# Layer 2's attention in an eight-block transformer kernel: the sums of weights taken one row a head, inverted there and spread by a product

## The chip, the core and the metric

The kernel runs on one core of a Trainium2 chip. The time is the device time of one execution, in microseconds (us); the lower the better. A core has a matmul engine (TensorE, PE in the profile, with its weight loads as PEld), a vector engine (VectorE, DVE), a scalar engine (ScalarE, ACT), a general engine (GpSimd, POOL) and an engine that issues transfers (SyncE, SP). Each takes its instructions from a list of its own, in order; they wait for each other by semaphores. SBUF is the memory on the chip, PSUM the small memory that TensorE writes to, in eight banks of 128 x 512 float32.

## The reference

All of it is float32. The input `x` has 128 sequences of 64 tokens of 128 numbers (8192 tokens), with a context of the same 128 x 64 tokens of 96 numbers. Eight blocks follow each other (four attentions, four feed-forward layers), each added to `x` through a gate. The change touches one, layer 2's attention with 16 heads of 8 numbers, which sees a normalised `x` as `query` and the context as `key_value`:

```python
q = (query @ Wq + bq).reshape(B, Nq, H, D).transpose(0, 2, 1, 3)
k = (key_value @ Wk + bk).reshape(B, Nkv, H, D).transpose(0, 2, 1, 3)
v = (key_value @ Wv + bv).reshape(B, Nkv, H, D).transpose(0, 2, 1, 3)
attn = jnp.einsum('bhqd,bhkd->bhqk', q, k) * scale
attn = jnp.clip(attn, -CLAMP, CLAMP)
attn = jax.nn.softmax(attn, axis=-1)
attn = jnp.where(jnp.any(jnp.isnan(attn)), jnp.asarray(1.0 / Nkv, attn.dtype), attn)
x = jnp.einsum('bhqk,bhkd->bqhd', attn, v).reshape(B, Nq, Cq)
return x @ Wo + bo
```

Each sequence attends to its own 64 context tokens. The softmax's division is done late in the kernel: the weights are exponentials, the products with `v` are taken of these, and what comes out is divided by the sum of the weights of its head and query.

## The kernel before, in words

`l2_cross` (from line 788) is a software pipeline written out by hand. A unit `u` is four sequences, 256 tokens ("a pair" of token tiles; 32 of them, `NP`); a group `g` is two units (16, `NG`). `PLAN` (line 967) is the order of work in one period; `period(i)` goes through it and calls each step for unit `i + lag`, the steps of kind "g" only where that number is even, for group (i + lag) / 2. All engines' instructions are recorded through `InOrder` (line 158), which ties each to the one before it on its engine, so `PLAN` is the order on every engine. Line 166 issues them all, so the profile names that line for every instruction, and one goes by the names of the tiles.

The steps of one period `i`, with what each puts on which engine:

- `count` and `clamp` (unit i): ACT takes a sum of exponentials of the raw scores `sc`, to see later whether any is not a number; DVE clamps the scores from PSUM into `s`, in two halves.
- `norm` (unit i+4): ACT normalises two tiles into `xn`; for odd units POOL then adds the gated bias to `x`.
- `heads` (unit i-3): TensorE multiplies the turned weights `aT` with `vz`, which holds the values of each head in otherwise empty columns, into the left half (256 columns) of a bank `pso`: row 8h+d is head h, number d, and the columns are the 256 tokens. Then it multiplies `aT` with `hot_v`, ones at the places of a head, into the right half: there all eight rows of a head get the same sum.
- `qk` (group of even i): projections `psq`, `psk`, copied by ACT to `qT`, `kT`.
- `power` (unit i-1): ACT's exponential of `s`, in two halves.
- `values` (unit i-2): projection `psv`. `turn` (unit i-2), halves 0 and 1: TensorE transposes the weights, two banks `psa` a half; ACT copies each to `aT`. Between the halves `scores` (unit i+1) on TensorE, from `qT` and `kb`.
- `transposes` (odd i): `psx`, copied by ACT to `xT`.
- `largest` (unit i): DVE's maximum `m` of each row of `s`; `less` (unit i): POOL subtracts it, in two halves.
- `place` (unit i-2): DVE copies `psv` into `vz` (two copies).
- `spread` (unit i+2): POOL makes `kb`, each key repeated by head under a mask, in two halves.
- `divide` (unit i-3): DVE inverts the right half of `pso` (128 x 256) to `rec` and multiplies the left half with it into `oT_all`.
- `statistics` (even i): DVE's mean and variance of four tiles, then four small steps on POOL (`rs`, `rr`, `nb` twice).

So even periods have `qk` and `statistics`, odd ones `transposes` and the bias. The `pso`, `psq`, `psk`, `psv`, `psa` and `psx` tiles share four banks of PSUM (`bank`, line 63), each taken by the next tile when its last user is done; the scores have the other four.

After the last scores three more periods empty the pipeline; between them `groups` puts the output projection `psf` and its addition to `x`, and `ahead` runs the first steps of the next layer. `l2_ffn` (line 1037) follows: 32 experts with top-8 routing, whose router's small tiles `m8`, `gt`, `eq` have two buffers each.

```python
        PLAN = [
            ("u", 0, count, 0), ("u", 0, clamp, 1), ("u", 4, norm), ("u", 0, clamp, 0), ("u", 0, count, 1),
            ("u", -3, heads), ("g", 2, qk), ("u", -1, power, 0), ("u", -1, power, 1),
            ("u", -2, values), ("u", -2, turn, 0), ("u", 1, scores), ("u", -2, turn, 1), ("g", 3, transposes),
            ("u", 0, largest), ("u", 0, less, 0), ("u", 0, less, 1), ("u", -2, place), ("u", 2, spread),
            ("u", -3, divide), ("g", 6, statistics),
        ]
```

Of the kernel before, what the change touches and what calls it, by code (L numbers as in the profile page):

```python
# [9 lines left out]
F32 = mybir.dt.float32  # L10
# [3 lines left out]
ALU = mybir.AluOpType  # L14
AX = mybir.AxisListType

P = 128
NB, SQ, DM = 128, 64, 128
# [9 lines left out]
class Cols:  # L28
# [13 lines left out]
    "l0f": Cols(qa=8 * 128, qb=8 * 128, va=8 * 64, vb=8 * 64, o=8 * 128, sim=16, st=64),  # L42
    "l1x": Cols(**XA),
    "l1f": Cols(re=128, im=128, dc=128, ds=128, dn=128),
    "l2x": Cols(q=128, k=128, v=128, o=128, bq=1, bd=4),
    "l2f": Cols(gw=32, g=2048, u=2048, d=2048, sg=128, su=128, sd=128),
    "l3x": Cols(q=1024, k=1024, v=1024, o=1024, gn=1, nv=1),
    "l3f": Cols(u1=32, v1=512, u2=128, v2=128, b1=4),
# [6 lines left out]
def flamingo_kernel(ctx: ExitStack, tc: tile.TileContext, a: dict, out: bass.AP):  # L55
# [116 lines left out]
    dve, actor, gps, mat, sp = engines = [InOrder(e) for e in (vec, act, pool, pe, nc.sync)]  # L172
# [615 lines left out]
    def l2_cross(ahead):  # L788

        stack = ExitStack()  # L790
        keep = ctx.enter_context(opened("l2x_v", 1, RIGHT))
# [4 lines left out]
        w = views(w_t, "l2x")  # L796
# [3 lines left out]
        v = keep.tile([P, 4, 4, 2, 32], F32, name="vz")  # L800
        gps.memset(v, 0.0)

        hot = keep.tile([P, 2, 32], F32, name="hot_v")
        gps.memset(hot, 0.0)
        for r in range(2):
            for j in range(2):
                gps.memset(hot[r * 64:(r + 1) * 64, j, 16 * j + 8 * r:16 * j + 8 * r + 8], 1.0)
        wv = w["v"].rearrange("p (c r d) -> p r c d", r=2, d=8)
        yield True

# [7 lines left out]
        ps = bank("psvm")  # L818
# [4 lines left out]
        sg, su = [{} for _ in range(NG)], [{} for _ in range(NP)]  # L823
# [109 lines left out]
        def turn(u, t):  # L933
            aT = su[u]["aT", t] = wk2.tile([P, 8, P], F32, tag="aT", name=f"aT_l2x_{u}_{t}")
            for i in range(2):
                ps = bank(f"psa_l2x_{u}_{t}_{i}")
                for j in range(4):
                    h = 2 * (4 * i + j)
                    mat.transpose(ps[:, j * P:(j + 1) * P],
                                  su[u]["s"][:, t, h:h + 2, :].rearrange("p h k -> p (h k)"), ident)  # L940
                actor.copy(aT[:, 4 * i:4 * i + 4, :].rearrange("p j q -> p (j q)"), ps)

        def heads(u):

            ps = su[u]["o"] = bank(f"pso_l2x_{u}")
            for t in range(2):
                for b in range(2):
                    for j in range(2):
                        for c in range(4):
                            mat.matmul(ps[32 * c:32 * c + 32, t * P + b * 64:t * P + b * 64 + 64],  # L950
                                       lhsT=v[:, 2 * t + b, c, j, :],
                                       rhs=su[u]["aT", t][:, 2 * c + j, b * 64:(b + 1) * 64],
                                       start=j == 0, stop=j == 1)
            for t in range(2):
                for j in range(2):
                    for c in range(4):
                        mat.matmul(ps[32 * c:32 * c + 32, 256 + t * P:256 + (t + 1) * P],
                                   lhsT=hot[:, j, :], rhs=su[u]["aT", t][:, 2 * c + j, :], start=j == 0, stop=j == 1)

        def divide(u):  # L960
            rec = wk2.tile([P, 256], F32, tag="rec", name=f"rec_l2x_{u}", bufs=1)
            dve.reciprocal(rec, su[u]["o"][:, 256:512])
            dve.tensor_tensor(oT[:, u * 256:(u + 1) * 256], su[u]["o"][:, 0:256], rec, ALU.mult)
            su[u].clear()


        PLAN = [
            ("u", 0, count, 0), ("u", 0, clamp, 1), ("u", 4, norm), ("u", 0, clamp, 0), ("u", 0, count, 1),
            ("u", -3, heads), ("g", 2, qk), ("u", -1, power, 0), ("u", -1, power, 1),
            ("u", -2, values), ("u", -2, turn, 0), ("u", 1, scores), ("u", -2, turn, 1), ("g", 3, transposes),  # L970
            ("u", 0, largest), ("u", 0, less, 0), ("u", 0, less, 1), ("u", -2, place), ("u", 2, spread),
            ("u", -3, divide), ("g", 6, statistics),
        ]
# [63 lines left out]
    def l2_ffn(ahead):  # L1037
        w = W["l2f"]
        BIG = 3.0e38
        ahead().step()  # L1040
        with opened("l2f_0", 2, RIGHT) as fr:
# [42 lines left out]

            def groups(g):

                ch, m8, gs = new(g, "ch", [P, 4, 32]), new(g, "m8", [P, 16, 8]), new(g, "gs", [P, 4, 4])
                dve.tensor_tensor(ch, st[g]["sc"], bc(row["gb"], 1, 4), ALU.add)
                c8 = ch.rearrange("p t (g e) -> p (t g) e", e=8)
                for i in range(16):  # L1090
                    dve.max(m8[:, i, :], c8[:, i, :])
                dve.tensor_tensor(gs.rearrange("p t g -> p (t g)"), m8[:, :, 0], m8[:, :, 1], ALU.add)

            def best_groups(g):

                gs = st[g]["gs"]
                gt, eq, rank = new(g, "gt", [P, 4, 4, 4]), new(g, "eq", [P, 4, 4, 4]), new(g, "rank", [P, 16])
# [372 lines left out]
def _layout(i):  # L1470
    f = {}
    f["x"] = i["x"].reshape(NT, P, DM).transpose(1, 0, 2).reshape(P, NT * DM)
    f["ctxT"] = np.concatenate([i["ctx_768"].reshape(NTOK, DC).T, np.ones((1, NTOK), np.float32)])
    for name, key in (("m0", "mask_BxS2_bk0"), ("m1", "mask_BxS2_bf1")):
# [21 lines left out]
    f["l1f"] = _pack("l1f", re=i["L1_ffn_w_freq_real"], im=i["L1_ffn_w_freq_imag"],  # L1496
                     dc=np.cos(ang), ds=np.sin(ang), dn=-np.cos(ang))

    f["l2x"] = _pack("l2x", q=i["L2_xattn_Wq"],
                     k=np.concatenate([i["L2_xattn_Wk"], i["L2_xattn_bk"][None]]),  # L1500
                     v=np.concatenate([i["L2_xattn_Wv"], i["L2_xattn_bv"][None]]), o=i["L2_xattn_Wo"],
                     bq=i["L2_xattn_bq"][:, None], bd=np.tile(np.repeat(np.eye(4), 8, axis=0), (4, 1)))
# [42 lines left out]
```

## Time and profile before

Three runs took 3132.29, 3133.40 and 3134.66 us, median 3133.4. The profiled execution took 3130.18 us, its span from the first to the last instruction is 3128.4 us, and the mean granted TensorE clock is 0.988 of full speed.

| | whole kernel, us | share | stretch 1307 to 1506 us (199 us) |
|---|---|---|---|
| TensorE matmul | 2976.4 | 95% | 172.3 |
| TensorE weight load | 1968.2 | 63% | 124.9 |
| VectorE | 1931.2 | 62% | 190.9 |
| ScalarE | 1561.4 | 50% | 182.8 |
| GpSimd | 1261.2 | 40% | 176.6 |

The stretch in the last column lies within layer 2's attention, which goes from its first scores at 1289 us to its last projection at 1605 us. In the page's strip of 40 slices these are slices 16 to 20, the only ones in which DVE, ACT and POOL are busy together.

Some groups of the stage, by tile:

| tile | engine | shape | times | us each |
|---|---|---|---|---|
| `rec_l2x` | DVE reciprocal | 128 x 256 | 32 | 1.758 |
| `oT_all` | DVE product | 128 x 256 | 32 | 0.424 |
| `m_l2x` | DVE maximum | 128 x 2048 to 32 | 32 | 2.286 |
| `s_l2x` from `sc` | DVE clamp | 128 x 1024 | 64 | 1.212 |
| `vz` | DVE copy | 64 x 256 | 64 | 0.419 |
| `aT_l2x` | ACT copy | 128 x 512 | 128 | 0.600 |
| `s_l2x` | POOL `less` | 128 x 1024 | 64 | 1.902 |
| `kb_l2x` | POOL `spread` | 128 x 512 | 64 | 1.048 |
| `pso` from `hot_v` | PE | 128 x 128, 32 rows out | 1024 | 0.273 |

A matmul of float32 stands as two records in the trace, and its duration is that of one in a pipeline, so several overlap. A busy share is an average over a stretch; which engine sets the pace is read from the chain of waits within it. In a timeline row the columns are start, length, engine, line, operation, tiles and shape, count, and in brackets the idle time before it with what ended that.

### The profile page before, as it was taken

How to read it: one execution, taken by the hardware profiler on the slowest of the kernel's cores; microseconds unless marked ns; L12 is line 12 of the kernel's file. 1: busy time of each engine (PE TensorE's matmuls, PEld its weight loads, DVE VectorE, ACT ScalarE, POOL GpSimd, SP SyncE). 2: the span in 40 equal slices, each digit the busy share in tenths (PEclk: the TensorE clock that was granted, in tenths of full speed). 3: DMA queues.
4: the chain of work that ended last, by engine and by line, in shares of the span. 5: the costliest groups of instructions: out<-in, count | busy, mean ns of one | idle time of the engine just before them, and what ended most of it. 6: DMA issues, size and time to landing. Idle time of an engine off the chain costs nothing.

```text
span 3128.4 us, 79938 instructions
## 1 busy us (share of the span) xinstructions
PE 2976.4 (95%) x34018; PEld 1968.2 (63%) x34018; DVE 1931.2 (62%) x4494; ACT 1561.4 (50%) x2756; POOL 1261.2 (40%) x1439
## 2 busy tenths in 40 slices
PE   8999899999999999788879999999999999999998
PEld 7888644444458888566644444444447888888883
DVE  5666666656646667699964444444445666666664
ACT  5666432222236666699723233233225666666655
POOL 3444311111014444688624444444443333333353
PEclk9999999999999999899999999999999999999999
DMA  5000455655620000000034534534520000000001
GB/s 152 2 3 2 98 135 122 135 131 115 135 65 3 3 2 3 29 3 3 3 71 94 109 69 96 107 66 101 107 57 14 3 2 2 3 3 3 3 2 55
DMA packets 89511, 164.92 MB, mean 53 GB/s; under 512 B 8929, under 2 KB 20833, under 8 KB 88193
## 3 DMA queue, kind: packets, MB, share of 16 engines
q1 hardware_dynamic: 89154, 159.81, 22.8%
q8 instruction: 267, 4.37, 0.6%
q14 instruction: 90, 0.74, 0.1%
HBM read 154.00 MB, written 5.77 MB: 51 GB/s over the span
## 4 chain that ended last, share of the span: by engine, by line
PE 79%; DVE 15%; ACT 2%; POOL 2%; issue 1%; DMA 0%; DVEq 0%; SPq 0%; ACTq 0%; POOLq 0%
PE psgu_l2f L166 12%; PE psqkv_l0f L166 11%; PE psy_l2f L166 5%; PE psv_l3x L166 4%; PE pso_l3x L166 4%; PE psq_l3x L166 4%; PE psy_l0f L166 4%; PE psk_l3x L166 4%; PE sc_l3x L166 2%; PE psa_l3x L166 2%; DVE m_l2x L166 2%; DVE s_l2x L166 2%; PE o_l3x L166 2%; PE psv_l1x L166 2%; PE psq_l1x L166 2%; PE pso_l1x L166 2%
## 5 line engine op out<-in xcount | busy, mean ns | idle before, releaser
L166 PE MATMUL psgu_l2f<-xT_l2f,w_l2f 128*128 128x512 f32 x1088 | 512.8, 594 | 0.1
L166 POOL TENSOR_TENSOR h_l2f<-uw_l2f,sl_l2f 128x512 f32<-128x512 f32 x256 | 325.1, 1270 | 408.8 <-DVE uw_l2f L166 408.8
L166 DVE TENSOR_TENSOR uw_l2f<-psgu_l2f,wb_l2f 128x512 f32<-128x512 f32 x256 | 176.2, 689 | 361.3 <-ACT sl_l2f L166 361.3
L166 ACT ACTIVATE sl_l2f<-psgu_l2f 128x512 f32<-128x512 f32 x272 | 162.4, 597 | 466.2 <-PE psgu_l2f L166 461.6
L166 PE MATMUL psqkv_l0f<-xs_l0f,w_l0f 128*128 128x512 f32 (+1 forms) x1024 | 350.5, 600 | 3.5 <-DVE xs_l0f L166 3.5
L166 PEld LDWEIGHTS psgu_l2f<-xT_l2f,w_l2f 128*128 128x128 f32 x1088 | 202.4, 191 | 237.5 <-issue 222.3
L166 PE MATMUL psy_l2f<-h_l2f,w_l2f 128*128 128x512 f32 x544 | 277.7, 593 | 0.0
L166 PEld LDWEIGHTS psqkv_l0f<-xs_l0f,w_l0f 128*128 128x128 f32 (+1 forms) x1024 | 125.2, 164 | 188.7 <-issue 177.9
L166 POOL TENSOR_TENSOR at_l3x<-s_l3x,rec_l3x 128x1024 f32<-128x1024 f32 x64 | 121.8, 1903 | 166.5 <-DVE rec_l3x L166 156.9
L166 PEld LDWEIGHTS psy_l2f<-h_l2f,w_l2f 128*128 128x128 f32 x544 | 103.5, 190 | 129.5 <-issue 125.2
L166 POOL TENSOR_SCALAR rs_l0f<-mv_l0f 128x4 f32<-128x4 f32 x16 | 16.1, 1004 | 369.9 <-DVE mv_l0f L166 369.9
L166 DVE TENSOR_REDUCE den_l3x<-s_l3x 128x16 f32<-128x1040 f32 x64 | 79.1, 1235 | 132.1 <-ACT s_l3x L166 132.1
L166 DVE TENSOR_TENSOR xs_l0f<-wb_l0f,xT_l0f 128x1024 f32<-128x1024 f32 x128 | 151.4, 1214 | 2.5 <-PE psqkv_l0f L166 1.1
L166 POOL TENSOR_TENSOR x<-x,gbias_b 128x256 f32<-128x256 f32 (+1 forms) x80 | 68.0, 850 | 205.9 <-DVE ln_xn_l1x L166 107.6
L166 PE MATMUL psq_l3x<-xT_l3x,w_l3x 128*128 128x256 f32 x512 | 136.3, 389 | 0.0
L166 POOL TENSOR_TENSOR s_l2x<-s_l2x,m_l2x 128x1024 f32<-128x1024 f32 x64 | 120.4, 1902 | 33.2 <-DVE m_l2x L166 25.4
L166 PE MATMUL psk_l3x<-ctxT,w_l3x 96*128 96x256 f32 x512 | 133.1, 382 | 0.0
L166 PEld LDWEIGHTS pso_l3x<-w_l3x,oT_l3x 128*128 128x128 f32 x1024 | 126.0, 194 | 4.5 <-ACT oT_l3x L166 1.3
L166 DVE TENSOR_TENSOR s_l3x<-sc_l3x,maskf_m 128x512 f32<-128x512 f32 x128 | 82.4, 686 | 75.2 <-PE sc_l3x L166 75.2
L166 PE MATMUL pso_l3x<-w_l3x,oT_l3x 128*128 128x128 f32 x1024 | 126.6, 278 | 1.2 <-ACT oT_l3x L166 1.2
L166 PE MATMUL psv_l3x<-w_l3x,ctxT 97*64 97x256 f32 x1024 | 124.7, 386 | 0.0
L166 PE MATMUL psy_l0f<-mix_l0f,w_l0f 128*128 128x512 f32 x256 | 114.3, 599 | 0.0
(562 smaller groups left out, 6639.8 us busy)
## 6 DMA issues: line engine op xcount, KB each, us to landing
wb_l0f<-wrow_l0f SPq DMA_DIRECT2D x256, 256.0 KB, 5.6
wb_l2f<-wrow_l2f SPq DMA_DIRECT2D x128, 512.0 KB, 9.1
out_dram<-x SPq DMA_DIRECT2D x16, 256.0 KB, 2.6
w_l2f<-in_l2f_dram SPq DMA_DIRECT2D x1, 3280.0 KB, 11.6
w_l0f<-in_l0f_dram SPq DMA_DIRECT2D x1, 2088.0 KB, 27.3
w_l3x<-in_l3x_dram SPq DMA_DIRECT2D x1, 2049.0 KB, 7.8
x<-in_x_dram SPq DMA_DIRECT2D x1, 2048.0 KB, 18.6
ctxT<-in_ctxT_dram SPq DMA_DIRECT2D x1, 1536.0 KB, 23.6
```

The source lines that it names most:

```text
L166: got = getattr(self.eng, op)(*args, **kwargs)
```

## The change

In `heads` the sums are taken into 64 columns instead of 256. The weights `hot` are windows of a block of ones and zeros that now comes with the layer's weights: the product for `aT` column block `a` and quarter (t, b) of the tokens goes to rows 64t + 32b to +32, of which rows h and 16 + h are both the sum of head h. So the 128 rows hold the 16 heads of each of the four sequences, twice, and the columns the 64 tokens of a sequence. It is 32 products of 64 columns where there were 16 of 128.

A new step `invert` follows at once: DVE inverts these 128 x 64 sums, and POOL multiplies the result, repeated four times, with a mask `own` (128 x 4) that leaves each sequence's rows in its own 64 columns. A new step `expand` after `turn`'s second half: TensorE multiplies that 128 x 256 tile with `ex` (128 x 128, zeros and ones, using the first 16 of each 32 rows), which puts each head's row on its eight rows of output, into the right half of `pso`. `divide` now has ACT copy that half to `oT_all`, and DVE multiply the left half with it in place.

In `turn` the first of a unit's four copies of `aT` is on DVE and no longer on ACT. `PLAN` gets `invert` behind `heads` and `expand` behind the second `turn`. The fills that made `hot_v` are gone; the layer's weights have 711 columns instead of 517. In `l2_ffn` the tiles `m8`, `gt` and `eq` have one buffer each.

```diff
-    "l2x": Cols(q=128, k=128, v=128, o=128, bq=1, bd=4),
+    "l2x": Cols(q=128, k=128, v=128, o=128, bq=1, bd=4, hot=62, ex=128, own=4),
...
-        hot = keep.tile([P, 2, 32], F32, name="hot_v")
-        gps.memset(hot, 0.0)
-        for r in range(2):
-            for j in range(2):
-                gps.memset(hot[r * 64:(r + 1) * 64, j, 16 * j + 8 * r:16 * j + 8 * r + 8], 1.0)
+        hot = [w["hot"][:, 30 - 2 * a:62 - 2 * a] for a in range(8)]
...
-                actor.copy(aT[:, 4 * i:4 * i + 4, :].rearrange("p j q -> p (j q)"), ps)
+                copy = dve.tensor_copy if t == i == 0 else actor.copy
+                copy(aT[:, 4 * i:4 * i + 4, :].rearrange("p j q -> p (j q)"), ps)
...
-            for t in range(2):
-                for j in range(2):
-                    for c in range(4):
-                        mat.matmul(ps[32 * c:32 * c + 32, 256 + t * P:256 + (t + 1) * P],
-                                   lhsT=hot[:, j, :], rhs=su[u]["aT", t][:, 2 * c + j, :], start=j == 0, stop=j == 1)
+            for a in range(8):
+                for t in range(2):
+                    for b in range(2):
+                        c0 = 64 * t + 32 * b
+                        mat.matmul(ps[c0:c0 + 32, 256:320], lhsT=hot[a],
+                                   rhs=su[u]["aT", t][:, a, b * 64:(b + 1) * 64], start=a == 0, stop=a == 7)
+
+        def invert(u):
+            rec = wk2.tile([P, SQ], F32, tag="rec", name=f"rec_l2x_{u}", bufs=1)
+            dve.reciprocal(rec, su[u]["o"][:, 256:320])
+
+            own = su[u]["own"] = wk2.tile([P, 4, SQ], F32, tag="own", name=f"own_l2x_{u}", bufs=1)
+            gps.tensor_tensor(own, bc(rec, 1, 4), bc(w["own"], 2, SQ), ALU.mult)
+
+        def expand(u):
+
+            mat.matmul(su[u]["o"][:, 256:512], lhsT=w["ex"], rhs=su[u]["own"].rearrange("p a q -> p (a q)"),
+                       start=True, stop=True)
...
         def divide(u):
-            rec = wk2.tile([P, 256], F32, tag="rec", name=f"rec_l2x_{u}", bufs=1)
-            dve.reciprocal(rec, su[u]["o"][:, 256:512])
-            dve.tensor_tensor(oT[:, u * 256:(u + 1) * 256], su[u]["o"][:, 0:256], rec, ALU.mult)
+            cols = slice(u * 256, (u + 1) * 256)
+            actor.copy(oT[:, cols], su[u]["o"][:, 256:512])
+            dve.tensor_tensor(oT[:, cols], su[u]["o"][:, 0:256], oT[:, cols], ALU.mult)
             su[u].clear()
...
-            ("u", -3, heads), ("g", 2, qk), ("u", -1, power, 0), ("u", -1, power, 1),
-            ("u", -2, values), ("u", -2, turn, 0), ("u", 1, scores), ("u", -2, turn, 1), ("g", 3, transposes),
+            ("u", -3, heads), ("u", -3, invert), ("g", 2, qk), ("u", -1, power, 0), ("u", -1, power, 1),
+            ("u", -2, values), ("u", -2, turn, 0), ("u", 1, scores), ("u", -2, turn, 1), ("u", -3, expand), ("g", 3, transposes),
...
-                ch, m8, gs = new(g, "ch", [P, 4, 32]), new(g, "m8", [P, 16, 8]), new(g, "gs", [P, 4, 4])
+                ch, m8, gs = new(g, "ch", [P, 4, 32]), new(g, "m8", [P, 16, 8], bufs=1), new(g, "gs", [P, 4, 4])
```

More of the change, by code (lines that the diff above doesn't have):

```diff
@@ L1096, in best_groups @@
                 gs = st[g]["gs"]
-                gt, eq, rank = new(g, "gt", [P, 4, 4, 4]), new(g, "eq", [P, 4, 4, 4]), new(g, "rank", [P, 16])
+                gt, eq = (new(g, k, [P, 4, 4, 4], bufs=1) for k in ("gt", "eq"))
+                rank = new(g, "rank", [P, 16])
                 gm = new(g, "gm", [P, 16], U8)
@@ L1497, in _layout @@
                      dc=np.cos(ang), ds=np.sin(ang), dn=-np.cos(ang))
+    ones, heads = np.zeros((2, 64, 62)), np.zeros((32, P))
+    for r in range(2):
+        ones[r, :, [30 + r, 46 + r]] = 1
+    for h in range(16):
+        heads[h, 8 * h:8 * h + 8] = 1
     f["l2x"] = _pack("l2x", q=i["L2_xattn_Wq"],
@@ L1501, in _layout @@
                      v=np.concatenate([i["L2_xattn_Wv"], i["L2_xattn_bv"][None]]), o=i["L2_xattn_Wo"],
-                     bq=i["L2_xattn_bq"][:, None], bd=np.tile(np.repeat(np.eye(4), 8, axis=0), (4, 1)))
+                     bq=i["L2_xattn_bq"][:, None], bd=np.tile(np.repeat(np.eye(4), 8, axis=0), (4, 1)),
+                     hot=ones.reshape(P, 62), ex=np.tile(heads, (4, 1)), own=np.repeat(np.eye(4), 32, axis=0))
     f["l2f"] = _pack("l2f", gw=i["L2_ffn_gate_w"].T,
```

## The prediction

> **What bounds the kernel now.** The page's chain of waits is TensorE for 79% of the whole kernel, but the edit sits in one stage, so I read that stage by itself. The starts of the 32 reductions `m_l2x`, one a pair, run from 1294.43 to 1546.46 us. From pair 4 to pair 26 (1325.79 to 1506.99) two pairs take 16.41 us nearly every time. The table of stretches over one such double period:
>
> ```profile
> 1407.83:1424.60 16.77, 14.23 (x329) 10.33 (x328) 16.04 (x22) 15.18 (x27) 14.78 (x14) 1.00 0.01 3
> ```
>
> The columns after the length are PE, PEld, DVE, ACT, POOL, clock, DMA. DVE is busy 16.04 of 16.77, ACT 15.18 and POOL 14.78: four queues are close to full, and DVE is the fullest. The chain of waits in the stage is DVE alone; one pair:
>
> ```profile
> 1405.47 2.27 DVE s_l2x L166 x2
> ...
> 1407.83 2.29 DVE m_l2x L166
> ...
> 1410.96 1.77 DVE rec_l2x L166
> ...
> 1412.75 0.42 DVE oT_all L166
> 1413.18 0.78 DVE sts_l2x L166 x4
> ```
>
> So today nothing but DVE's own work sets the pace: clamp, reduce, `vz` copies, reciprocal, product. Next, the timeline of POOL over an even pair and into the odd one:
>
> ```profile
> 1410.27 3.76 POOL L166 TENSOR_TENSOR s_l2x<-s_l2x,m_l2x 128x1024 f32<-128x1024 f32 x2 [1.60 <-DVE m_l2x L166]
> 1413.98 2.06 POOL L166 TENSOR_TENSOR kb_l2x<-kT_l2x,w_l2x 128x512 f32<-128x512 f32 x2
> 1416.12 0.23 POOL L166 TENSOR_SCALAR rs_l2x<-mv_l2x 128x4 f32<-128x4 f32 x1
> 1416.44 1.04 POOL L166 TENSOR_TENSOR rr_l2x<-rs_l2x,nhalf 128x4 f32<-128x4 f32 x1
> ...
> 1418.05 1.27 POOL L166 TENSOR_TENSOR x<-x,gbias_b 128x512 f32<-128x512 f32 x1
> 1419.37 3.76 POOL L166 TENSOR_TENSOR s_l2x<-s_l2x,m_l2x 128x1024 f32<-128x1024 f32 x2
> ```
>
> The reader should see that POOL, once it has the even pair's maximum (reduce over at 1407.83 + 2.29 = 1410.12), has no gap for 9.25 us, until 1419.37. Today nobody waits for the end of that run except the next `less`. Last, TensorE and ACT around the odd pair's end:
>
> ```profile
> 1403.77 0.60 PE L166 MATMUL psx_l2x<-cst_t,xn_l2x 128*128 128x128 f32 x4
> 1405.52 1.10 PE L166 MATMUL pso_l2x<-aT_l2x,vz 128*32 128x64 f32 x64 [1.15 <-DVE oT_all L166]
> ...
> 1409.96 0.77 PE L166 MATMUL psa_l2x<-cst_t,s_l2x 128*128 128x128 f32 x5
> ```
> ```profile
> 1404.45 0.59 ACT L166 COPY xT_l2x<-psx_l2x 128x512 f32<-128x512 f32 x1
> 1404.93 1.04 ACT L166 ACTIVATE junk<-sc_l2x 128x1024 bf16<-128x1024 f32 x1
> ```
>
> From the start of `heads` to the first transposes of `turn` behind it (through `qk` and `values`) TensorE needs 1409.96 - 1405.52 = 4.44 us; from the `psx` transposes to ACT's `xT` copy pass 0.7 to 0.8.
>
> **The change, part by part, for each pair.**
>
> *DVE.* The reciprocal shrinks from 128x256 (1.76 us) to 128x64. Rows: 128x16 takes 253 ns, so 6.27 ns an element, so 0.55 us for 64. A copy 128x512 out of PSUM is added: 128x256 took 0.42 and the clamp 128x1024 took 1.21, so about 0.67. The final product stays at 0.42. Sum -1.76 + 0.55 + 0.67 = -0.54 us a pair, -1.08 a double period, if no wait is added.
>
> *ACT.* One `aT` copy less (pitch about 0.5 in a row of four); one 128x256 copy more, which took 0.37 as `vd_l0f`. About -0.1 to -0.2.
>
> *TensorE.* The 32 records of 128 columns that gave the sums (first to last 0.84 us by their weight loads) become 64 of 64 columns; 64 records of that shape with `vz` took 0.94. So +0.1. The spreading product, K=128 by 256 columns, is two records at 0.27 each (`psq_l3x`: 136.3 us by 512): +0.53.
>
> *POOL.* `own`, 128x256 with two spread operands, has no row. Half of `kb` 128x512 (1.05) is 0.52 from below; the `x` addition 128x256, 0.744, is above. The line through `kb` and `s_l2x` (1.90 for 1024) gives 0.62, which I take as `kb` is the same operation. POOL's work becomes 14.78 + 2 x 0.62 + two gaps of 0.05 = 16.1 a double period: just within today's 16.41.
>
> *Memory and the rest.* The five small fills of `hot_v` on POOL (0.1 each, before the stage) go; the weight load on SP is 0.1 MB longer, and is issued a layer earlier. `m8`, `gt` and `eq` with one buffer are written and read by DVE alone, so their order on DVE already covers them: zero. If that cover failed it would be one 1.2 us group of maxima a token group, in a layer where TensorE is the bound.
>
> **The waits it adds, which decide.** In the changed program's order: (1) DVE's product of the pair waits for ACT's new copy, which stands last in ACT's list, in odd pairs behind the `xT` copy; the next pair's clamps queue behind that product. (2) The spreading product waits for `own`; queued behind it on TensorE are `psx` (odd pairs) and then the next `heads`, `qk`, `values`, `turn`. (3) `own` of an odd pair stands on POOL behind the even pair's `less`, the `kb`, the four statistics steps and the `x` addition, that is at the end of the 9.25 us run shown above. (4) DVE's `aT` copy waits for `turn`'s first transposes, and the reduction is queued behind it.
>
> These close a loop from one even maximum to the next, every link in strict order:
>
> - POOL from the even maximum to `own`: 9.25, and `own` 0.67 with its gap: 9.92
> - to TensorE 0.07, spreading product 0.55: 10.54
> - `psx` 0.47, then `heads` to `turn` 4.44 + 0.06 for the new sums: 15.51
> - four transposes until a copy may start (1402.66 to 1403.36 on ACT): 0.70
> - DVE's copy 0.70, reduction 2.29 + 0.05: 19.25 us
>
> Against 16.41, +2.84 a double period. The parallel branch through ACT (from `psx`: 0.79 until `xT`, 0.48, the new copy 0.28, count 1.0, norm 0.77, count 0.95, `qT` 0.74 = 5.01) arrives with TensorE's 4.97, so neither shortens it. POOL now idles some 3 us in the even pair.
>
> Bounds of the unknowns within the loop: `own` 0.52 to 0.76, spreading 0.43 to 0.6, the DVE copy 0.6 to 0.72: together -0.3 to +0.25 a double period, so -4 to +3 us in all.
>
> *How often.* The whole loop holds while there are statistics, additions and transposes ahead: even pairs 2 to 24. In the first, TensorE is at half clock (0.50 in the rows from 1302 to 1312): pair 2's first `turn` transposes start at 1310.26 and take about 1.2 at that clock until a copy may start, the copy 0.7, so the reduction goes from 1307.82 to about 1312.2 (+4.4); and 19.25 takes the place of 17.97 after it (+1.3): +5.7 in all. Then 11 double periods at 2.84, less 0.7 for two that took 16.77 before: +30.5. From pair 26 on the statistics (1.93 of POOL's run) are gone, the loop is 17.3 against 15.73 (+1.6); from pair 28 on there is no `psx` either and DVE's work decides, some 15.3 against 16.08 (-0.8), and -0.3 for the last pair: +0.5. In the three last passes the chain sums, reciprocal, `own`, spread, copy, product stands in the open: 0.55 + 0.62 + 0.65 + 0.37 + 0.42 + four handovers of 0.1, about 3.0, against 1.76 + 0.42 (but in two of them `turn` covers most): +0.5, +0.65, +0.85 = +2.0. Sum without the clock: +38.7.
>
> *The clock.* The loop leaves TensorE idle for about 2.2 us before each odd spreading product (`own` is done 9.9 after the even maximum; `turn` is over at 7.8: DVE's `vz` copies, product, statistics and first clamp to 3.75, ACT's count to 4.85, two exponentials to 6.7, one copy to 7.3, four transposes). The rows of the stage's end:
>
> ```profile
> 1546.30:1549.70 3.40, 0.85 (x6) 0.95 0.00 0
> 1549.70:1553.10 3.40, 0.79 (x5) 0.50 0.02 5
> ...
> 1566.80:1570.20 3.40, 1.57 (x12) 1.00 0.00 0
> ```
>
> A stretch of 3.4 us with 0.85 us of matmul was followed by half clock; so were ones with 1.13 and 1.27 (from 1583.5 and 1594.2). One with 1.57 was not. In the new loop a stretch of 3.4 us ending between 8.9 and 11.2 would hold under 1.3: 2.3 of 3.4, if the stretches run free, about two in three. Each costs 1.2 to 1.7 us (half of the 2.4 to 3.4 us of TensorE work that then runs at half speed). I take 6 of the 12 at 1.45: +8.7; ends 0 and 20.
>
> The Trainium skill ("TensorE: Matmul & The Clock Gate", Part 1) says that the clock halves after at least one idle window of about 3.4 us. Read strictly, 2.2 us of idling never trips it and the sum would stay at +38.7; the rows above show it tripped by windows that held 0.85 to 1.27 us of work, so the measurement decides.
>
> Sum: 38.7 + 8.7 = +47.4. Against the profiled execution (3130.18, span 3128.4) that is 3177.6; the median of the runs lies 3.2 above that execution, so 3133.4 + 47.4 = 3181.
>
> **The rivals.**
>
> - *Same loop, clock kept* (chance 0.22): +38.7, 3172. For: no stretch of full idleness. Against: the three rows.
> - *POOL gets `own` out early enough, only (1) and (4) remain* (0.17). Odd pair, from the end of `vz` to the product's end: 0.1 + 0.79 + 0.48 + 0.37 + 0.1 + 0.42 = 2.26, the same as today's 1.76 + 0.42 and gaps, so its reciprocal's saving is lost and 0.55 + 0.67 = +1.22 stays; even pair +0.18. +1.4 instead of 2.84: 4.3 + 15.4 - 0.7 + 2.5 = +21.5, 3155. Against: POOL's run of 9.25 us has no gap.
> - *The waits stay hidden and the change does what it says* (0.05): DVE's -1.08 or, where POOL's 16.1 holds, -0.3 a double period; over 12, -13 to -4: 3120 to 3130. It decides if `own` reaches TensorE before `turn` of its pair ends, 7.8 us after the even maximum; the row says 9.9.
> - A loop longer still, with every even pair's clock halved and more (0.04): above 3196.
>
> **How the numbers follow.** The forecast has 0.52, by itself 3170 to 3193. Its sides: the lower one reaches past the case with the clock kept into the case of 3155; the upper one takes all 12 halved periods at 1.3. Range 3156 to 3196. A measurement of this kernel can tell about 0.2% (6.3 us) from no change: faster 0.03, within 0.02, slower 0.95, all of the first two from the hidden-waits rival.
>
> **What would show it.** Reductions of even pairs about 19.2 us apart (or 20.7 with half clock); POOL waiting some 3 us for `m_l2x`; TensorE waiting about 2 us for POOL `own` in odd pairs; DVE waiting for ACT `oT_all` in odd pairs and under 1 us for `psa` in even ones; DVE busy share of the stage falling from 0.96 to about 0.8; rows of 0.5 in the clock. Wrong if the even reductions stay within 17 us, or if `own` costs far from 0.62.

## The result, and the profile after

The changed kernel takes 3179.77 us, the median of four runs (3175.59 to 3183.15), beside 3134.03 us for the kernel before on the same chip (3132.29 to 3138.57). The ratio is 1.0141, 95% interval [1.0128, 1.0154]: slower by 1.3 to 1.5%. The profiled execution took 3175.59 us, its span is 3173.8 us.

The engines' busy times on the page after:

```profile
PE 3008.7 (95%) x35106; PEld 1992.9 (63%) x35106; DVE 1906.9 (60%) x4526; ACT 1558.0 (49%) x2756; POOL 1279.8 (40%) x1466
```

VectorE has 24 us less to do (1931.2 before), and the kernel is 45.4 us longer. The stretch from 1330 to 1550 us, inside the stage, in the table of stretches (columns: length, PE, PEld, DVE, ACT, POOL, clock, DMA share, GB/s):

```profile
1330.00:1550.00 220.00, 179.90 (x4223) 131.57 (x4222) 156.88 (x262) 161.67 (x291) 167.11 (x163) 0.92 0.01 3
```

The same stretch in the kernel before:

```profile
1330.00:1550.00 220.00, 188.40 (x4399) 138.31 (x4392) 213.52 (x278) 200.79 (x355) 186.47 (x163) 1.00 0.01 3
```

VectorE is busy 156.9 of 220 us, 71%, where it was at 97% (213.5). No engine is close to full any more. So the stage is now held by a loop of waits. The view of waits of the same stretch (us in total, times, longest) names its members:

```profile
POOL s_l2x L166 <- PE pso_l2x L166: 46.7, 11, 4.4
DVE oT_all L166 <- ACT oT_all L166: 38.6, 10, 4.1
...
PE pso_l2x L166 <- POOL own_l2x L166: 22.5, 11, 2.1
DVE aT_l2x L166 <- PE psa_l2x L166: 22.3, 12, 2.2
```

Ten to twelve of each in 220 us: once a double period. The first line puts POOL's wait down to TensorE. The timeline shows that it is VectorE's maximum that came just before, as it must be, since `less` subtracts that:

```profile
1426.45 0.62 POOL L166 TENSOR_TENSOR own_l2x<-rec_l2x,w_l2x 128x256 f32<-128x256 f32 x1
...
1427.12 0.90 PE L166 MATMUL pso_l2x<-own_l2x,w_l2x 128*128 128x256 f32 x2 [2.08 <-POOL own_l2x L166]
...
1428.81 1.93 PE L166 MATMUL pso_l2x<-aT_l2x,vz 128*32 128x64 f32 x64
...
1429.81 0.42 DVE L166 TENSOR_TENSOR oT_all<-pso_l2x,oT_all 128x256 f32<-128x256 f32 x1 [3.96 <-ACT oT_all L166]
...
1434.24 1.09 PE L166 MATMUL psa_l2x<-cst_t,s_l2x 128*128 128x128 f32 x8
1434.93 0.69 DVE L166 COPY aT_l2x<-psa_l2x 128x512 f32<-128x512 f32 x1 [1.97 <-PE psa_l2x L166]
...
1435.54 2.28 DVE L166 TENSOR_REDUCE m_l2x<-s_l2x 128x32 f32<-128x2048 f32 x1
...
1437.89 3.76 POOL L166 TENSOR_TENSOR s_l2x<-s_l2x,m_l2x 128x1024 f32<-128x1024 f32 x2 [4.24 <-PE pso_l2x L166]
```

Read it downwards as one chain: `own` comes off POOL, the spreading product starts 0.05 us later after 2.08 us of nothing on TensorE, then `heads`, `qk`, `values` and at 1434.24 `turn`; 0.69 us into it VectorE may copy, and behind the copy stands the maximum, over at 1437.82. POOL starts its next round at 1437.89, after 4.24 us of nothing. From one even maximum to the next it is 20.44 us, eleven times out of eleven between pairs 4 and 26; before it was 16.41.

The first line of `heads` (`pso` from `aT` and `vz`, at 1428.81) is worth a second look: its 64 records took 1.93 us where 1.10 is usual. The table of stretches in steps of 3.41 us over one double period shows why (seventh number from the left, ahead of the DMA share: the granted clock):

```profile
1403.61:1407.02 3.41, 1.32 (x10) 1.00 (x10) 1.78 (x3) 1.35 (x3) 3.24 (x6) 1.00 0.00 0
1407.02:1410.43 3.41, 3.41 (x82) 2.88 (x84) 1.03 (x2) 1.92 (x5) 3.41 (x3) 0.50 0.02 5
1410.43:1413.84 3.41, 3.41 (x84) 2.02 (x73) 2.12 (x3) 2.98 (x7) 2.55 (x3) 1.00 0.02 5
1413.84:1417.25 3.41, 3.41 (x52) 2.51 (x50) 2.76 (x2) 3.10 (x6) 0.00 (x0) 1.00 0.00 0
...
1424.07:1427.48 3.41, 1.33 (x10) 1.00 (x10) 1.76 (x3) 1.34 (x3) 3.25 (x6) 1.00 0.02 5
1427.48:1430.89 3.41, 3.41 (x86) 2.89 (x88) 1.08 (x2) 1.98 (x5) 3.41 (x3) 0.50 0.00 0
```

A stretch with 1.32 us of matmul, the one in which TensorE waits for `own`, is followed by 3.41 us at half clock. This repeats 20.48 us later, and from pair 3 on the stage has twelve stretches at half clock, each 3.41 us long, the first from 1325.10 and the last from 1550.38 us. They hold the spreading product, `psx` and `heads`, which stand in the loop.

### The profile page after: what moved, and what is told of

Same layout as the page of the kernel before. It is cut to its first block, busy times and chain, and to the rows that moved or that the text cites. A ratio compares the mean times of both kernels' runs of the same rounds, so it can differ in the third digit from the quotient of the medians.

```text
span 3173.8 us, 82169 instructions
## 1 busy us (share of the span) xinstructions
PE 3008.7 (95%) x35106; PEld 1992.9 (63%) x35106; DVE 1906.9 (60%) x4526; ACT 1558.0 (49%) x2756; POOL 1279.8 (40%) x1466
## 4 chain that ended last, share of the span: by engine, by line
PE 82%; DVE 8%; POOL 5%; ACT 2%; issue 2%; DMA 0%; SPq 0%; POOLq 0%; DVEq 0%; ACTq 0%
PE psgu_l2f L166 11%; PE psqkv_l0f L166 10%; PE psy_l2f L166 5%; PE psv_l3x L166 4%; PE pso_l3x L166 4%; PE psy_l0f L166 4%; PE psq_l3x L166 4%; PE psk_l3x L166 3%; PE sc_l3x L166 2%; PE psa_l3x L166 2%; PE pso_l2x L166 2%; PE o_l3x L166 2%; PE psv_l1x L166 2%; PE psq_l1x L166 2%; PE pso_l1x L166 2%
```

## The experiments

Eleven kernels ran. "Double period" is the usual distance between two even maxima from pair 4 to pair 26; "stage" is the time from the first maximum to the first product of the following layer (`psgu_l2f`). Ratios are to the kernel before on the same chip, where its median was 3133.0 to 3136.9 us, with 95% intervals. In e4, e8 and e9 some turns with half clock are 1.1 to 1.6 us longer; the means are 18.14, 17.71 and 18.17 us.

| kernel | double period, us | stage, us | median, us | ratio |
|---|---|---|---|---|
| before | 16.41 | 311.0 | 3134.0 | |
| changed | 20.44 | 361.2 | 3179.8 | 1.0141 [1.0128, 1.0154] |
| e1: `own` on DVE | 18.43 | 337.0 | 3156.6 | 1.0085 [1.0059, 1.0112] |
| e2: clock kept | 18.85 | 348.9 | 3175.4 | 1.0131 [1.0114, 1.0148] |
| e3: all `aT` on ACT | 17.41 | 323.5 | 3148.5 | 1.0049 [1.0033, 1.0066] |
| e4: e1 and e3 | 17.76 | 329.9 | 3156.3 | 1.0067 [1.0046, 1.0089] |
| e5: no `own` | 17.51 | 328.5 | 3158.5 | 1.0077 [1.0062, 1.0092] |
| e6: e5, `aT` on ACT, new order | 16.95 | 321.6 | 3141.3 | 1.0017 [1.0008, 1.0027] |
| e7: e6, one `aT` of 8 on DVE | 16.95 | 319.2 | 3144.1 | 1.0028 [1.0011, 1.0045] |
| e8: e7, `psx` and copy moved | 17.41 | 335.4 | 3153.5 | 1.0059 [1.0042, 1.0076] |
| e9: e6, the same moves | 17.78 | 338.1 | 3159.1 | 1.0078 [1.0061, 1.0095] |
| e10: e7, only `psx` moved | 16.46 | 318.6 | 3140.7 | 1.0014 [0.9999, 1.0029] |
| e11: e8, last product earlier | 16.72 | 316.2 | 3135.3 | 1.0007 [0.9995, 1.0018] |

The stage is the sharper measure. What lies outside it took between 2810.4 and 2826.2 us in these profiled executions, and that difference goes with the clock: half clock outside the stage made up 33 us in the shortest (e11) and 64 in the longest (e8; changed: 33 us and 2812.6; before: 43 and 2817.4; e2: 61 and 2825.7). Executions of one kernel differ by as much with no edit between them (e10: 3127.5 to 3145.8 us).

### First set: each suspected wait by itself

**e1_own_dve.** One line: the product that makes `own` goes from POOL to DVE.

```diff
-            gps.tensor_tensor(own, bc(rec, 1, 4), bc(w["own"], 2, SQ), ALU.mult)
+            dve.tensor_tensor(own, bc(rec, 1, 4), bc(w["own"], 2, SQ), ALU.mult)
```

> The product `own` is made by DVE and no longer by POOL; all else as in the changed kernel. Theory (the loop goes through POOL's list): `own` is ready 0.45 us after the reciprocal, TensorE no longer waits for POOL, and what is left is DVE's own round with its waits for ACT's new copy: odd pair 2.36 clamps + 0.55 + 0.45 + 0.65 copy + 2.29 + 0.83 + 2.26 until the product is out = 9.4, even pair 8.85, together about 18.2 us instead of 20.44; the half clock goes too, since TensorE no longer stands still for 2 us. 12 double periods: about -26 us, 3148 to 3160. Rival (POOL's place in the chain is a bystander, DVE's own load and waits set the time): DVE gets 2 x 0.45 us more, +11 us, about 3190.

Measured: 18.43 us a double period, the clock at 1.00 from 1400 to 1500 us, and 24 us of the stage's 50 given back. The time is in the theory's range and far below the rival's 3190. With `own` off the end of POOL's run the long loop is gone, though VectorE, the busiest engine of the kernel before, has one more operation in each pair. That operation was itself a surprise (last section). How much of the 2.0 us a loop is the clock, e2 tells.

**e2_warm.** The changed kernel with four spare products, of a constant, into the columns that the spreading product of an odd pair then overwrites. They fill TensorE's wait for `own`.

```diff
         def expand(u):
+            if u % 2 == 0:
+                for _ in range(4):
+                    mat.matmul(su[u]["o"][:, 256:512], lhsT=w["ex"], rhs=cst_t[:, 0:256], start=True, stop=True)
```

(A pair that is worked on in an odd period has an even number, since `expand` lags by three.)

> Four spare 128x256 products into the right half of `pso` before the spreading product of each odd period; they wait for nothing and are overwritten by it. They fill the 2 us in which TensorE stands still with work. Theory (the half clock lengthens the loop from 18.85 to 20.44): the clock stays at 1.00 in the stage, the path from the spreading product to the next `turn` shrinks from 7.1 to 5.5 us, double period about 18.9, so -19 us: about 3161. Rival (the half clock falls on work that has slack): no gain, 3180, or up to +7 us where the spare products end after `own` is ready.

The timeline of e2 shows the spare products over before `own` comes, so that they delay nothing, and `heads` at its usual length:

```profile
1423.56 1.89 PE L166 MATMUL pso_l2x<-cst_t,w_l2x 128*128 128x256 f32 x8
...
1425.13 0.61 POOL L166 TENSOR_TENSOR own_l2x<-rec_l2x,w_l2x 128x256 f32<-128x256 f32 x1
...
1425.80 0.70 PE L166 MATMUL pso_l2x<-own_l2x,w_l2x 128*128 128x256 f32 x2 [0.35 <-POOL own_l2x L166]
...
1426.87 1.10 PE L166 MATMUL pso_l2x<-aT_l2x,vz 128*32 128x64 f32 x64
```

The double period is 18.85 us, 1.59 less, and the clock 1.00 throughout the middle of the stage. So the half clock costs 1.59 us a loop, and 18.85 is the loop of waits by itself. From pair 4 to pair 26 that is 17.4 us; behind pair 26 some 5.5 are lost again, and the stage is 12.3 us shorter. The median is only 4.4 us below that of the changed kernel: the profiled execution of e2 had 28 us more of half clock outside the stage. So the expected loop was met, and the expected time of 3161 us missed by 14.

e2 also puts the other edits in proportion, since they take away the half clock together with a link of the loop. Beside 18.85 us, e1's 18.43 is a gain of only 0.42 us a loop (but e1 also gives VectorE the product `own` in each pair); e3 and e5 below, at 17.41 and 17.51, gain 1.44 and 1.34.

**e3_act_copy.** The fourth of the `aT` copies goes back to ACT.

```diff
-                copy = dve.tensor_copy if t == i == 0 else actor.copy
-                copy(aT[:, 4 * i:4 * i + 4, :].rearrange("p j q -> p (j q)"), ps)
+                actor.copy(aT[:, 4 * i:4 * i + 4, :].rearrange("p j q -> p (j q)"), ps)
```

> All four `aT` copies on ACT again; all else as in the changed kernel. Theory (the reduction queues on DVE behind a copy that waits for `turn`, which is the last link of the loop): the reduction follows the reciprocal at once, the loop runs only through `psx`, `xT`, ACT's new copy, the product and the clamps. Even pairs' last transposes now wait for the `vz` copies, so odd `vz` end some 10.8 us after the even maximum; from there 0.8 + 0.5 + 0.4 + 0.8 + 2.4 + 0.6 + 2.3: about 18.3 us a double period instead of 20.44, and the stage's second pair doesn't wait 4.4 us at its cold start: -25 - 4, about 3150. Rival (the copy on DVE costs what it takes, 0.65 us a pair, or helps ACT): -21 us at most by its own time where DVE is the bound, 0 or a few us slower where ACT is.

17.41 us, better than expected, and 38 of the 50 us of the stage: the largest gain that a single undone part gave. The maximum no longer waits for `turn`, so the loop is cut at its other end. What remains is in the view of waits of e3, 1400 to 1500 us:

```profile
DVE oT_all L166 <- ACT oT_all L166: 25.6, 12, 2.2
```

Twelve times in 100 us, so in every pair, VectorE waits 2.1 us for ScalarE's new copy, with the next clamps queued behind.

**e4_both.** Both edits together.

> `own` on DVE and all four `aT` copies on ACT: only the shorter sums, the spreading product and the handover through ACT's copy are left of the change. Theory: the only wait left is the product behind ACT's copy, 2.2 us after the `vz` copies in odd and even pairs alike, the same 2.2 us that the long reciprocal and the product took before; so the shorter reciprocal saves nothing, and 0.55 + 0.45 stand on top in each pair: 16.41 + 2.0 = 18.4 a double period, about 3150. Rival (with both gone the change does what it says, DVE loses 1.76 and gets 1.0 a pair): 16.41 - 1.5, 3115.

17.65 to 17.76 us, and 18.8 to 19.0 in the four of eleven turns with a half clock: not better than e3 alone. The time, 3156 us, is above the theory's 3150 and far above the rival's 3115. The hope that the change pays once both waits are gone falls. With `own` on DVE and all copies on ACT, ACT is busy 54.2 of 60 us (1400 to 1460 us), and the wait for the copy of the spread reciprocals stands.

### Second set: can the shorter reciprocal be had without the waits?

**e5_slices.** `own` is left out: the spreading product becomes four of 64 columns, each with weights that hold only its own sequence's rows, and takes `rec` itself. The result is the same.

```diff
-            gps.tensor_tensor(own, bc(rec, 1, 4), bc(w["own"], 2, SQ), ALU.mult)
...
-            mat.matmul(su[u]["o"][:, 256:512], lhsT=w["ex"], rhs=su[u]["own"].rearrange("p a q -> p (a q)"),
-                       start=True, stop=True)
+            for a in range(4):
+                mat.matmul(su[u]["o"][:, 256 + 64 * a:320 + 64 * a], lhsT=w["ex"][:, a * P:(a + 1) * P], rhs=su[u]["rec"],
+                           start=True, stop=True)
...
-                     ex=np.tile(heads, (4, 1)), own=np.repeat(np.eye(4), 32, axis=0))
+                     ex=np.kron(np.eye(4), heads))
```

(The expectation says by a slip that GpSimd keeps the reciprocal; it is on VectorE, as in the changed kernel, and GpSimd has no part in the spreading. From here on the router's `ch` has one buffer too, and `ex` has 512 columns.)

> The changed kernel without the product `own`: the spreading is four products of 64 columns, each with its own sequence's four rows of `heads` and with the reciprocal `rec` as the moving operand, so GpSimd has the reciprocal alone (0.55 us) and nothing of GpSimd's work stands between the even maximum and the spreading product but that. The copy of `aT` on VectorE stays. Theory (only the place of `own` in GpSimd's queue costs the long loop): the odd pair needs `rec` before the even pair's two subtractions, as the kernel before needed its reciprocal; a double period of 17.0 to 17.6 us at full clock, the stage 10 to 22 us longer than before, the time 3142 to 3157 us. Rival (the loop is set by the spreading product itself, by its place ahead of `turn` in TensorE's order): 18.4 us or more, as with `own` on VectorE, 3156 us or more.

17.51 us and a stage 17.5 us longer than before, as the theory had it. The spreading product is at the same place in TensorE's order as in e1, and the period is 0.92 us below e1's; so this place alone does not hold 18.4 us, as the rival had it. The time, 3158.5, is a little above the theory's range and no help in choosing, as the rival named 3156 or more; half clock outside the stage was 58 us against 43 before.

**e6_plan_act** and **e7_plan_one.** e5, and the order of the steps turned so that each engine has other work before what it must wait for: `largest` ahead of `heads`, `place` ahead of the second `turn`, VectorE's last product (`last`) a pair later than the copy it needs, but for the final four pairs. e6 has all `aT` copies on ACT, e7 one of eight on DVE.

```diff
-            ("u", -3, heads), ("u", -3, invert), ("g", 2, qk), ("u", -1, power, 0), ("u", -1, power, 1),
-            ("u", -2, values), ("u", -2, turn, 0), ("u", 1, scores), ("u", -2, turn, 1), ("u", -3, expand), ("g", 3, transposes),
-            ("u", 0, largest), ("u", 0, less, 0), ("u", 0, less, 1), ("u", -2, place), ("u", 2, spread),
-            ("u", -3, divide), ("g", 6, statistics),
+            ("u", -3, heads), ("u", -4, last), ("u", 0, largest), ("u", -3, invert), ("g", 2, qk),
+            ("u", -1, power, 0), ("u", -1, power, 1), ("u", -2, values), ("u", -2, turn, 0), ("u", 1, scores),
+            ("u", -2, place), ("u", -2, turn, 1), ("u", -3, expand), ("g", 3, transposes),
+            ("u", 0, less, 0), ("u", 0, less, 1), ("u", 2, spread), ("u", -3, divide), ("g", 6, statistics),
```

> The spreading of four products without `own`, all four copies of `aT` on ScalarE, and the plan turned so that no engine waits for another's last step: `largest` ahead of the heads, the last product on VectorE (`oT_all` by the spread reciprocals) one pair later than the copy on ScalarE that it needs, `place` before the second turn. Theory (what the change lost are three waits, and what it saves, the shorter reciprocal on GpSimd, is real): the double period falls to the load of the busiest engine, ScalarE by its rows some 15.8 us; 15.8 to 16.5 us, the time 3120 to 3135 us. Rival (a bound of another kind holds the double period, the shorter reciprocal is worth nothing): 16.9 us or more, 3142 us or more.

> As the kernel with the turned plan, but one of the eight `aT` copies of a double period (the second half's second, odd pairs) on VectorE, behind its maximum rather than ahead of it. Theory (ScalarE is the bound once the waits are gone, so 0.7 us taken from it counts, and VectorE has room): 0.2 to 0.6 us less a double period than with all on ScalarE, 15.4 to 16.2 us, the time 3117 to 3132 us. Rival (every copy of `aT` on VectorE delays its maximum and with it GpSimd): 0.5 us more a double period, 3126 us or more.

Both have 16.95 us: the rival's number for e6, and for e7 neither. The times, 3141 and 3144 us, are above the theories' ranges. The stretch from 1400 to 1500 us of e6:

```profile
1400.00:1500.00 100.00, 92.38 (x2445) 73.03 (x2444) 79.02 (x130) 92.59 (x173) 85.06 (x78) 1.00 0.01 3
```

VectorE is down from 97 to 79 of 100 us, and nothing is won by it. ScalarE, at 92.6, has 15.7 us of work a double period and still waits. That moving one copy from ACT to DVE (ACT then has 89.6 us of 100) leaves the period as it is says that ACT's load is not the bound either: another loop holds the 16.95 us.

### Third set: which wait holds the turned order

**e8_plan_b** and **e9_plan_c.** e7 and e6 with `transposes` moved ahead of the second `turn` (in e9 ahead of `scores`), and ACT's copy to `oT_all` moved behind the next pair's counts, VectorE's last product behind the maximum.

```diff
-            ("u", -3, heads), ("u", -4, last), ("u", 0, largest), ("u", -3, invert), ("g", 2, qk),
+            ("u", -4, late_copy), ("u", -3, heads), ("u", 0, largest), ("u", -4, last), ("u", -3, invert), ("g", 2, qk),
...
-            ("u", -2, place), ("u", -2, turn, 1), ("u", -3, expand), ("g", 3, transposes),
+            ("g", 3, transposes), ("u", -2, place), ("u", -2, turn, 1), ("u", -3, expand),
```

> The kernel with the turned plan and one `aT` copy of eight on VectorE, but in TensorE's order `transposes` stand ahead of the second turn rather than behind the spreading product, and ScalarE's copy of the spread reciprocals to `oT_all` comes behind the next pair's two counts. Theory (the 16.95 us are held by ScalarE's two waits, 1.2 us for `psx` and 0.2 us for `pso` a double period, and by VectorE's second clamp, which waits 1.0 to 1.4 us a pair for the count that stands behind them): 15.6 to 16.5 us a double period, 3115 to 3130 us, level with or faster than before. Rival (another loop of the same length lies beside it): 16.8 us or more, 3135 to 3147 us.

> As the run beside it, with all `aT` copies on ScalarE and `transposes` ahead of the scores as well. Theory (ScalarE's load, some 15.9 us by its rows, is then the bound): 15.9 to 16.7 us a double period, 3118 to 3133 us. Rival (a loop of the same length as with the first turned plan): 16.8 us or more, 3135 to 3147 us.

Both are slower than what they started from (17.41 and 17.78 us): the theory falls, the rivals' bound of 16.8 us holds, and the times are above even the rivals'. The rivals left the loop unnamed; the timeline of e9 names the new wait in it:

```profile
1431.45 2.29 DVE L166 TENSOR_REDUCE m_l2x<-s_l2x 128x32 f32<-128x2048 f32 x1
...
1433.66 0.41 DVE L166 TENSOR_TENSOR oT_all<-pso_l2x,oT_all 128x256 f32<-128x256 f32 x1
...
1434.13 0.66 PE L166 MATMUL psa_l2x<-cst_t,s_l2x 128*128 128x128 f32 x4 [1.76 <-DVE oT_all L166]
```

No data goes from `oT_all` to `psa`. TensorE waits for a bank of PSUM: `pso` holds one of the four that `psa` and it share until the last product has read it, and that product now stood behind 2.29 us of maximum. (The next two expectations call the wait 1.76 us a pair. In the stretch from 1400 to 1500 us TensorE waited 8.8 us in five times in e8, once a double period, and 11.1 us in eleven times in e9, 1.0 us a pair.)

**e10_psx_early** takes back everything but the move of `transposes`; **e11_last_first** keeps all of e8, but puts the last product ahead of `heads` and of the maximum.

```diff
-            ("u", -4, late_copy), ("u", -3, heads), ("u", 0, largest), ("u", -4, last), ("u", -3, invert), ("g", 2, qk),
+            ("u", -4, late_copy), ("u", -4, last), ("u", -3, heads), ("u", 0, largest), ("u", -3, invert), ("g", 2, qk),
```

> The first turned plan with one `aT` copy of eight on VectorE, and one step moved: `transposes` stand ahead of the second turn in TensorE's order; the copy to `oT_all` and the last product stay where that plan had them, so that the heads' bank is free as early. Theory (the two plans before this one were slow because the last product, behind the maximum, kept the heads' bank, for which the next `turn` waited 1.76 us a pair; with the bank free only ScalarE's 1.2 us wait for `psx` is taken away): 16.0 to 16.6 us a double period, 3122 to 3132 us. Rival (moving `transposes` is itself what made them slow, since psx then takes a bank between the two turns): 17.2 us or more, 3140 us or more.

> The plan with the copy to `oT_all` behind the next pair's counts, but the last product right behind that copy, ahead of the heads and of the maximum. Theory (the bank's hold, not the copy's place, was the cost): the wait of 1.76 us a pair is gone, the maximum comes some 0.8 us later after the clamps, a double period of 16.3 to 17.2 us, 3125 to 3145 us. Rival (the move of `transposes`, in both, is the cost): 17.2 us or more.

16.46 and 16.72 us, both within the theory's ranges and below the rivals': with the bank released early the loss is gone, and the move of `transposes` by itself gains 0.49 us a double period. Of the times, e11's 3135 us lies in its range, while e10's 3141 lies above the theory's 3122 to 3132 and where its rival had it; from pair 4 to pair 26 e10 takes 181.4 us as the kernel before takes 181.2, and most of the 7.6 us by which its stage is longer lie behind the last maximum (66.0 for 59.0 us). The times are level with the kernel before, 1.0014 [0.9999, 1.0029] and 1.0007 [0.9995, 1.0018]. The stretch of the kernel before, and then that of e10, to be read beside that of e6 above:

```profile
1400.00:1500.00 100.00, 86.38 (x1999) 62.90 (x2004) 97.34 (x134) 92.28 (x166) 87.87 (x80) 1.00 0.01 3
1400.00:1500.00 100.00, 95.02 (x2475) 74.75 (x2460) 85.00 (x142) 92.49 (x171) 87.65 (x79) 1.00 0.02 4
```

TensorE has become the fullest engine, at 95 of 100, and ScalarE is at 92.5. No version beat the kernel before. Whether another order gets below 16.4 us stays open.

## Why the prediction was right, and where its sizes were off

The forecast of 3181 us rested on one loop, from an even maximum through POOL's run to `own`, the spreading product, `heads` to `turn`, VectorE's copy and the next maximum. That loop is what the profile shows, link by link, and e1, e3 and e5 each shortened the period by cutting one link of it, also beside e2, which has the loop without the half clock. The terms of the sum, measured within the stage:

| term | predicted | measured |
|---|---|---|
| start, to pair 4 | +5.7 | +6.7 |
| 11 double periods, waits and clock | +30.5 and 11/12 of 8.7 | +43.6 |
| pairs 26 to 31 | +0.5 | -1.2 |
| tail | +2.0 and 1/12 of 8.7 | +1.1 |
| stage | +47.4 | +50.2 |
| outside the stage | 0 | -4.8 |

The zero for `m8`, `gt` and `eq` holds: from the first `psgu_l2f` to the start of the last `psy_l2f` the feed-forward layer took 753.3 us before and 753.5 after. The -4.8 us go with 10 us less of half clock outside the stage.

*The loop without the clock.* Predicted 19.25, measured in e2 18.85. By links, in e2 and in the changed kernel: POOL from the maximum to the end of `own` 9.70 (predicted 9.92); from there to `turn` 5.58 in e2 (5.59), and 7.17 in the changed kernel, where all of the half clock's 1.59 us falls; to the copy 0.69 (0.70); copy and maximum 2.89 (3.04). So the costs of the two operations without a row were well bounded: `own` took 0.615 us (0.62 predicted, 0.52 to 0.76), the copy on VectorE 0.69 at most (0.67), the reciprocal of 64 columns 0.549 (0.55), the copy on ScalarE 0.38 (0.37).

*The clock: the term that was mis-sized.* The prediction took 6 of 12 loops at 1.45 us, 8.7 in all, supposing that stretches of 3.4 us run free of the loop. It was 12 of 12, and 1.59 each, 19.1. This is 10.4 us too little, against 4.4 too much for the loop (11 times 0.40) and the 4.8 outside the stage, so that the sum came within 2 us partly by luck: with 19.1 us for the clock it would have been 38.7 + 19.1 = 57.8 us, 3191. (The upper side of the range, given as all 12 loops at 1.3, would by that reason be 3133.4 + 38.7 + 15.6 = 3188 and not 3196.)

Why all twelve: the stretches do run free, as supposed. In the record of the granted clock the half clock began at 1325.10, 1345.58, 1366.06 and so on to 1550.38 us, 20.48 apart each time, and every other beginning of half clock in that execution lies a whole multiple of 3.413 us from these. The loop with half clock is 20.44 us long, 0.04 less than six such stretches, so in eleven turns the wait for `own` moves only some 0.4 us against them and falls into nearly the same place each time. Nothing in the record shows that one ties the other; that the lengths come so close looks like chance. It fits that e4 and e9, whose turns of 17.65 to 17.78 us are 5.2 stretches long, took half clock in only one of three or four.

The Trainium skill ("TensorE: Matmul & The Clock Gate", Part 1) has windows of 3413 ns that run freely and a drop after a window of idleness. The first agrees with these beginnings. The second does not fit: of the twelve, ten were preceded by a stretch with 1.32 to 1.34 us of matmul in it, the others by 1.55 and 1.70. No threshold comes out of the rows: in the changed kernel's execution 1.58 us (from 1615.23) was followed by full clock and 2.12 us (from 3100.03) by half. One of the prediction's own rows of the kernel before, 1.27 us from 1594.2, overlaps the half clock that it is said to precede, which begins at 1597.14; the 3.41 us ahead of that hold 0.81. That the drop needs no full stretch of idleness stands without it, and e2, which fills the wait and keeps the clock, bears it out.

*What would show it.* The even reductions came 20.44 us apart (20.7 was named for a loop with half clock). TensorE's wait for `own` was 2.08 us (about 2 predicted). VectorE's wait for ScalarE's copy in odd pairs was there, at 3.9 us. The waits of POOL for the maximum (4.24, predicted about 3) and of VectorE for `psa` (1.97, predicted under 1) were larger, and VectorE's share smaller (0.71 for 0.8); in e2, at full clock, they are 2.96, 1.00 and 0.76, so most of that excess is the half clock again.

*The rivals.* The same loop with the clock kept is e2 by construction; its stage is 38 us longer than before, as that rival's +38.7 had it. That POOL gets `own` out early enough falls with the 9.70 us from the maximum to its end and TensorE's 2.08 us of waiting. A loop longer still was to stand above 3196 us; 3180 was measured. That the change does what it says once the waits are hidden is answered by e4 to e11: with the named waits taken away or shortened the time comes back to that of before, not below it. The saved VectorE time was real (97% down to 85% in e10) and bought nothing in any order that was tried. ScalarE, GpSimd and TensorE stood at 92, 88 and 86 us of 100 in the kernel before, which leaves little room; that this is why is argued, not shown, and which loop holds the last 16.46 us was not found.

## What to carry to other kernels

Here four engines were each near 90% busy, and taking work from the fullest won nothing, while the new hand-overs between them cost. So look at a hand-over's place in all four queues: follow it round until it comes back to where it began, and add up the loop. A short operation that is put at the end of a long run of another engine comes when that run is over: `own` is 0.62 us of work, and it ended 9.70 us after the maximum. When a step is moved later, look at what it holds meanwhile (here a bank of PSUM), and where a wait of TensorE leaves a stretch of 3.4 us with little matmul in it, add the half clock that may follow (here 1.59 us behind a wait of 2.08).

## What the runs showed that was not expected

On VectorE the product `own` (128x256, both operands in SBUF) took from 0.42 to 1.30 us in e1, median 0.68. The timeline of e1 has a long one:

```profile
1412.60 2.05 POOL L166 TENSOR_TENSOR kb_l2x<-kT_l2x,w_l2x 128x512 f32<-128x512 f32 x2
...
1413.76 1.17 DVE L166 TENSOR_TENSOR own_l2x<-rec_l2x,w_l2x 128x256 f32<-128x256 f32 x1
1414.74 0.28 POOL L166 TENSOR_SCALAR rs_l2x<-mv_l2x 128x4 f32<-128x4 f32 x1
```

It began while POOL was in the second of its two `kb` products and ended 0.28 us after that one, at 1414.93. Another, begun 0.65 us into such a product (at 1404.88), took 0.67 us and ended 0.27 us after it. In another double period an `own` of 0.46 us began 0.14 us ahead of the second product, and POOL's pair took 2.23 us instead of 2.05. So the two engines hold each other up. The Trainium skill ("SBUF — State Buffer", "SBUF: two separate sides") says that a VectorE operation with two inputs in SBUF and GpSimd share a pair of ports, and that whichever starts first holds it for its whole instruction. These rows agree, though `own`, 0.42 us when undisturbed, ended less than that after POOL's product. The clamps, copies and maxima of VectorE, with one input, kept their lengths beside POOL's work.
